# Layer 0's feed-forward and layer 1's attention of the first half, recorded as side chains of layer 0's attention

## The chip, the cores and the metric

The kernel runs on 1 core of one Trainium2 chip. The metric is the time of one execution on the device in microseconds (us); a figure without further words is the median of nine runs. A core has five engines with queues of their own: PE multiplies matrices (its weight loads are counted apart, as PEld), DVE works on vectors, ACT evaluates functions, POOL does general work and here issues indirect transfers, SP issues plain transfers. The working memory of 128 partitions is SBUF; PE writes into PSUM, from where DVE or ACT take the products.

## The reference

A sequence model of four layers in post-layernorm form: x becomes layernorm(x + attention(x)), then layernorm(x + feed-forward(x)), four times. x has 4 rows of 1024 steps of 128 numbers, in float32. Each layer has another attention and another feed-forward. The change touches the first half of these steps:

- Layer 0's attention projects x to values, a gate and a score (`in_proj`), runs a causal convolution of four taps along the sequence over them, takes the running sums along the sequence of exp(score), and of exp(score) times cosine and sine of value times four frequencies, with a decay for each of 32 heads; it divides the sums by the running sum of exp(score), scales each step by its root mean square, mixes with W_re and W_im, multiplies with the gate and projects out.
- Layer 0's feed-forward quantizes x and a weight to a 6-bit grid, each block of 32 numbers with a scale of its own, and multiplies:

```python
        scales = jnp.maximum(jnp.max(jnp.abs(blocks), axis=-1) / FP6_E2M3_MAX, eps)
        q = _nearest_on_grid(blocks / scales[..., None], _GRID)
```

  The result is (quantized x) times (quantized weight) transposed, plus a bias.
- Layer 1's attention is a diagonal complex recurrence along the sequence: an input product with B, a scan for the real and the imaginary part, an output product with C.
- Layer 1's feed-forward is a mixture of 16 experts. The router gives each token four experts out of the two best of four groups; their outputs are summed by weight, and a shared expert is added.

Layers 2 and 3 follow with a softmax attention, eight experts, a Toeplitz mixing and sixteen experts.

## The kernel before

x stays in SBUF as 32 tiles of 128 tokens by 128 numbers. The sequence is cut into four quarters of 256 steps; a quarter holds the steps of all four rows, so 1024 columns or eight tiles, and quarters depend on one another only through carried sums. Quarters 0 and 1 are the first half, called part `a`; quarters 2 and 3 are part `r` in layer 1.

`all` (from L1887) records the program. Its stages are written as generators which yield estimated costs. `run` records one to its end. `mix(main, side, pace, drain)` records a step of `main`, then as many steps of `side` as the yielded costs of `main` allow; the side's costs are multiplied by `pace` first, so that with 0.6 more of the side is recorded for the same step of `main`; with `drain` what is left of the side follows. Each instruction recorded from the side is tied (`queued`) behind the latest instruction of `main` on its engine. `chain` puts generators one after the other, `abreast` advances several together, `when` yields 1.0 at a time until a condition holds. A scheduler then fixes the order of every engine's queue while the program is built; on the chip an engine runs its queue in this order, and an instruction that waits holds up all behind it.

Up to the first experts the order of the stages is: layer 0's attention of quarters 0 and 1 (`l0_attn`), the set-up of layer 1's attention and of layer 2, the filling of layer 1's lists with zeros (`zero_lists`, transfers on SP), layer 0's feed-forward of quarters 0 and 1 (`l0_ffn`), layer 1's attention of both (`l1_attn`), the routing of these 2048 tokens (`l1_route`), then layer 0's attention of quarters 2 and 3 with the spread as its side. The spread (`spread`, L1313) is 64 indirect transfers issued by POOL (L1301): each scatters one tile of 128 tokens into the list of one of its four choices, at rows that `posl1a` names. After that the shared expert (`l1_shared`, which adds into x, and so waits for the scatters that read the same tiles of x) and the experts (`l1_experts`: L1332 fetches four tiles of a list on SP and waits for all 64 scatters; `gu` are its first products, `hg` its gated products at L1749) are mixed with layer 0's feed-forward and layer 1's attention of quarters 2 and 3. Then 64 gathers, again L1301, bring the experts' rows back as `yt`, and the kernel goes on to layer 2.

Within `l0_attn`, `prepare` forms `z` (projection and convolution as four accumulated products, psz at two buffers of two banks) and ACT turns it into values `xv`, gate `gate` and exponentials `pq`; `den` is the scan of the exponentials (L363). For each of four frequencies ACT makes cosine and sine, DVE multiplies and scans (`re`, `s`), and PE mixes the sums into `yv`. At the end DVE takes the reciprocal `rs` (L462), multiplies with the gate, and adds the product `po` to x; `norm` follows. `z2`, `ms` and `po` use the pool `side` of PSUM, two buffers for all. `quantize` (L477) works on 128x1024 numbers of a quarter with DVE (ri, st, r, dst) and POOL (v, d twice). In `l0_ffn` POOL adds the bias to x (L529), PE transposes the quantized tiles and multiplies, DVE adds into x. `l1_attn` takes half of its products with `pw` on POOL for the first half of the sequence (L667) and on DVE for the second. `norm` finds 1/sqrt with ACT's root and DVE's reciprocal (`by="act"`) or with an iteration on DVE (`by="dve"`); the second half's calls use the latter.

Of the kernel before, what the change touches and what calls it, by code (L numbers as in the profile page):

```python
# [15 lines left out]
ALU = mybir.AluOpType  # L16
# [4 lines left out]
P = 128  # L21
# [53 lines left out]
class Kernel:  # L75
# [291 lines left out]
    def l0_attn(self, qs):  # L367
# [6 lines left out]
        with ExitStack() as ctx:  # L374
            bp = self.pool(ctx, "l0b", 2)
            tp = self.pool(ctx, "l0t", 2)
            psz = self.pool(ctx, "l0z", 2, space=PSUM)
            psy = self.pool(ctx, "l0y", 1, space=PSUM)
            pss = self.side

            def prepare(q):
                z2 = self.tile(pss, [P, BLK], "s")[:, :TQ]
                for k in range(CK):
# [44 lines left out]
            for q in qs:  # L428
                xv, gate, den, pq = made.pop(q)
                ms = self.tile(pss, [P, BLK], "s")[:, :TQ]  # L430
                self.l0_by_head(ms, self.headd, den, True, False)
                yv = self.tile(psy, [P, QC], "yv")
                for m in range(MF):

                    t = self.tile(tp, [P, QC], "t")
                    nc.scalar.activation(t, xv, AF.Copy, scale=self.turn[:, m : m + 1])
                    k = self.tile(tp, [P, QC], "k")
                    nc.scalar.activation(k, xv, AF.Identity, scale=self.turn[:, m : m + 1], bias=self.rnd)
                    nc.vector.scalar_tensor_tensor(k, k, RND, t, ALU.subtract, ALU.subtract)
                    im = self.tile(tp, [P, QC], "im")  # L440
                    nc.scalar.activation(im, k, AF.Sin, scale=-2.0 * PI_IN)
                    nc.scalar.activation(k, k, AF.Abs)
                    re = self.tile(tp, [P, QC], "re")
                    nc.scalar.activation(re, k, AF.Sin, scale=-2.0 * PI_IN, bias=self.halfpi)
                    for part, v in ((1, im), (0, re)):
                        tt(v, v, pq, ALU.mult)
                        s = self.tile(tp, [P, QC], "s", bufs=3)
                        self.l0_scan(s, v, 2 * m + part, q)
                        sq = self.tile(tp, [P, QC], "sq")
                        nc.scalar.activation(sq, s, AF.Square)  # L450
                        first, last = m == 0 and part == 1, m == MF - 1 and part == 0
# [14 lines left out]
                for g in range(2):  # L466
                    po = self.tile(pss, [P, 4, D], "s")
                    for k in range(4):
                        t = g * 4 + k
                        self.mm(po[:, k, :], gate[:, t * P : (t + 1) * P], self.w_out)  # L470
                    t0 = q * QT + g * 4
                    tt(x[:, t0 : t0 + 4, :], po, x[:, t0 : t0 + 4, :], ALU.add)
                self.norm(self.quarter(q), by="act")
                yield (10.0,)


    def quantize(self, tp, dst, src, nblk):  # L477
# [10 lines left out]
        v = new()  # L488
        nc.gpsimd.tensor_tensor(v3(v), v3(src), ri.unsqueeze(2).to_broadcast(big), ALU.mult)

# [6 lines left out]

        d = new()
        nc.gpsimd.tensor_tensor(d, r, v, ALU.subtract)
        nc.vector.scalar_tensor_tensor(d, d, 2.0, st, ALU.mult, ALU.is_ge)  # L500
        nc.gpsimd.tensor_tensor(d, d, st, ALU.mult)
        nc.vector.tensor_tensor(r, r, d, ALU.subtract)
        nc.vector.tensor_tensor(v3(dst), v3(r), sc.unsqueeze(2).to_broadcast(big), ALU.mult)

    def l0_ffn(self, qs, beside=False):

        nc, tc, x = self.nc, self.tc, self.x
        with ExitStack() as ctx:
            tp = self.pool(ctx, "l0ft", 4, right=beside)
            qp = self.pool(ctx, "l0fq", 2, right=beside)  # L510
            ps = self.side if beside else self.pool(ctx, "l0fps", 2, space=PSUM)
            tag = lambda t: "s" if beside else t
            if qs[0] == 0:
                w = self.load(qp, self.ins["l0_w"])
                self.quantize(tp, w, w, D // 32)
                self.l0_wT = self.tile(self.l0, [P, D], "wT")
                self.transposes(ps, self.l0_wT, [w], tag=tag("tp"))
            for q in qs:
                t0 = q * QT
                xd = self.tile(qp, [P, QT, D], "xd")  # L520
                self.quantize(
# [6 lines left out]

                nc.gpsimd.tensor_tensor(  # L529
                    x[:, t0 : t0 + QT, :], x[:, t0 : t0 + QT, :],  # L530
                    self.row["l0_b"].unsqueeze(1).to_broadcast([P, QT, D]), ALU.add,
                )
                for g in range(2):
                    xdT = self.tile(qp, [P, BLK], "xdT")
                    self.transposes(ps, xdT, [xd[:, g * 4 + k, :] for k in range(4)], tag=tag("tp"))
                    po = self.tile(ps, [P, 4, D], tag("po"))
                    for k in range(4):
                        self.mm(po[:, k, :], xdT[:, k * P : (k + 1) * P], self.l0_wT)
                    s = slice(t0 + g * 4, t0 + g * 4 + 4)
                    nc.vector.tensor_tensor(x[:, s, :], po, x[:, s, :], ALU.add)  # L540
                    yield (4.0,)
                self.norm(self.quarter(q), by="dve" if beside else "act")
                yield (6.0,)
                for g in range(2):
                    self.turned(ps, t0 + g * 4, tag=tag("tp"))
                yield (4.0,)
# [76 lines left out]

    def l1_attn(self, qs, beside=False):
        nc, tc, x, xT = self.nc, self.tc, self.x, self.xT
# [4 lines left out]
        with ExitStack() as ctx:  # L630
            tp = self.pool(ctx, "l1t", 2, right=beside)
            ps = self.side if beside else self.pool(ctx, "l1ps", 2, space=PSUM)
            tag = lambda t: "s" if beside else t
            for q in qs:
                pu = []
                for h in range(2):
                    z = self.tile(ps, [P, BLK], tag("pu"))
                    self.mm(z, self.l1_b, xT[:, q * QC + h * BLK : q * QC + (h + 1) * BLK])
                    pu.append(z.rearrange("p (b t) -> p b t", b=B // 2))
                g = []  # L640
                for r in range(2):
# [4 lines left out]
                    if q:  # L646
                        tt(rows(b)[:, :, 0], rows(b)[:, :, 0], lh[:, r, :], ALU.add)
                    s = self.tile(tp, [P, QC], f"g{r}")
                    nc.vector.tensor_tensor_scan(
# [16 lines left out]

                (tt if beside else nc.gpsimd.tensor_tensor)(rows(g[0]), rows(g[0]), steps(pw[:, 0, :]), ALU.mult)  # L667
                tt(rows(g[1]), rows(g[1]), steps(pw[:, 1, :]), ALU.mult)
                for h in range(2):
                    po = self.tile(ps, [P, 4, D], tag("po"))  # L670
                    for k in range(4):
# [5 lines left out]
                    yield (3.0,)  # L677
                self.norm(self.quarter(q), by="dve" if beside else "act")
                yield (6.0,)
                for h in range(2):  # L680
                    self.turned(ps, q * QT + h * 4, tag=tag("tp"))
                yield (4.0,)
# [1204 lines left out]
    def all(self):  # L1887
# [259 lines left out]
```

## Time and profile before

| | |
|---|---|
| median of 9 runs | 2054.12 us (2047.82 to 2056.29) |
| the profiled execution | 2056.79 us, of which the profile's span is 2055.0 us, at a mean granted clock of PE of 0.87 |
| busy in the span: PE, PEld | 1542.0 us (75%), 935.0 us (45%) |
| DVE, ACT, POOL | 1263.8 us (62%), 823.9 us (40%), 728.4 us (35%) |

The part that the change touches is the first 610 us. By stretches of the span, with busy times in us:

| stretch (us) | what runs | PE | DVE | ACT | POOL |
|---|---|---|---|---|---|
| 0 to 31.5 | loads, set-up | 20.1 | 24.4 | 14.4 | 10.3 |
| 120 to 140.4 | end of attention, quarter 1 | 9.5 | 10.9 | 3.1 | 0 |
| 241 to 280 | layer 1's attention and routing, start of quarter 2 | 29.1 | 29.7 | 23.5 | 8.6 |
| 361.8 to 381.6 | end of attention, quarter 3 | 9.3 | 10.3 | 3.0 | 15.1 |
| 505 to 610 | gathers, the second half's feed-forward and attention | 64.9 | 67.2 | 27.7 | 69.0 |

The stretches that are left out, attention of quarters 0 and 1 (31.5 to 120), the feed-forward (140.4 to 197.5), layer 1's attention (197.5 to 241), attention of quarters 2 and 3 (280 to 361.8), the shared expert (381.6 to 425.2) and the experts (425.2 to 505), stand among the lines of the prediction. A busy time near the stretch's length says that the engine had work throughout; the rest is waiting. In a line of the timeline the first number is the start in the span, the second the duration; then come engine, source line, operation, the tile written and the tiles read with their shapes, and in brackets the idle time before it and what ended it. A "x8" at the end says that eight like instructions in a row are drawn together.

### The profile page before, as it was taken

Reading aid. Unit: us, or ns where it says so; the run is one execution under the profiler, and the core shown is the slowest. Engines: PE = TensorE matmul, PEld = TensorE weight load, DVE = VectorE, ACT = ScalarE, POOL = GpSimd, SP = SyncE. Lnnn points to the kernel's source line nnn. Section 1 sums busy time; section 2 is a strip of 40 time slices with the busy share of each in tenths; the row PEclk is TensorE's granted clock in tenths of the full one; section 3 lists DMA queues with packets and bytes.
Section 4 is the critical chain, followed back from the end, with each engine's and each line's share of the span. In section 5 each row is a group of like instructions: output and inputs, shape, how many; then the busy total and the mean of one; then the engine's idle time right before and its main releaser. Section 6 shows DMA issues by size and latency. Waiting matters only on the chain. (4 is left out here: it accounts for less than half of the span.)

```text
span 2055.0 us, 27036 instructions
## 1 busy us (share of the span) xinstructions
PE 1542.0 (75%) x9017; PEld 935.0 (45%) x9017; DVE 1263.8 (62%) x3630; ACT 823.9 (40%) x1180; POOL 728.4 (35%) x681
## 2 busy tenths in 40 slices
PE   7743777687948787989979797987989898368080
PEld 3322533376524344866633332335656686255070
DVE  8876699456766765636646676476563475347253
ACT  6821177133324443423347565662222254233050
POOL 2012168403650570174332000300247500755755
PEclk9876688799978997999989999998999899689595
DMA  9980000233440112532230000003151331232252
GB/s 310 288 233 0 0 27 34 91 103 124 134 164 33 49 67 95 182 118 70 69 129 24 1 1 1 22 1 144 47 210 69 106 117 34 79 107 67 75 157 58
DMA packets 215530, 187.10 MB, mean 91 GB/s; under 512 B 16528, under 2 KB 194064, under 8 KB 214864
## 3 DMA queue, kind: packets, MB, share of 16 engines
q1 hardware_dynamic: 194672, 142.29, 21.9%
q0 software_dynamic: 20704, 42.86, 6.4%
q8 instruction: 84, 1.38, 0.3%
q14 instruction: 70, 0.57, 0.1%
HBM read 88.49 MB, written 96.60 MB: 90 GB/s over the span
## 5 line engine op out<-in xcount | busy, mean ns | idle before, releaser
L1055 ACT ACTIVATE pr<-sc 128x1024 f32<-128x1024 f32 x288 | 279.1, 1021 | 214.8 <-PE sc L157 214.7
L157 PE MATMUL sc<-qm,kT 32*128 32x512 f32 (+3 forms) x1536 | 190.1, 549 | 0.9 <-ACT pr L1055 0.9
L157 PE MATMUL gu<-ld,xgT 128*128 x640 | 168.8, 408 | 26.5 <-DVE hg L1749 22.6
L157 PE MATMUL s<-pr,va 128*32 128x512 f32 (+3 forms) x1536 | 162.1, 518 | 19.7 <-DVE x L993 7.2
L157 PE MATMUL gu<-wall,xgT 128*128 x304 | 146.6, 607 | 2.7 <-ACT xgT L167 2.0
L157 PEld LDWEIGHTS gu<-ld,xgT 128*128 128x128 f32 x640 | 123.0, 203 | 52.6 <-DVE hg L1749 21.4
L1061 DVE TENSOR_TENSOR pr<-pr,ld 128x512 f32<-128x512 f32 (+1 forms) x160 | 92.2, 580 | 85.3 <-ACT pr L1055 84.8
L165 PE MATMUL tp<-ld,xg 128*128 128x128 f32 x396 | 66.7, 297 | 85.0 <-DMA xg<-l3rc 49.5
L157 PEld LDWEIGHTS sc<-qm,kT 32*128 32x128 f32 x1536 | 83.5, 193 | 93.6 <-issue 63.1
L1749 DVE TENSOR_TENSOR hg<-sg,gu 128x256 f32<-128x256 f32 x160 | 65.8, 417 | 93.8 <-ACT sg L1748 93.2
L167 ACT COPY xgT<-tp 128x512 f32<-128x512 f32 x99 | 57.9, 585 | 163.1 <-PE tp L165 163.1
L169 DVE COPY hT<-tp 128x512 f32<-128x512 f32 x118 | 80.9, 685 | 68.6 <-PE tp L165 68.5
L1301 POOL DMA_INDIRECT l1ra<-x,posl1a x64 | 93.0, 1454 | 59.5 <-DVE posl1a L1276 40.2
L1748 ACT ACTIVATE sg<-gu 128x256 f32<-128x256 f32 x160 | 61.0, 384 | 121.7 <-PE gu L157 96.8
L165 PE MATMUL tp<-ld,hg 128*128 128x128 f32 x624 | 98.0, 277 | 7.1 <-DVE hT L169 3.6
L165 PEld LDWEIGHTS tp<-ld,hg 128*128 128x128 f32 x624 | 78.2, 142 | 54.2 <-issue 32.5
L1507 ACT ACTIVATE sg<-gu 128x512 f32<-128x512 f32 x76 | 45.4, 598 | 139.3 <-PE gu L157 130.5
L1301 POOL DMA_INDIRECT l1rr<-x,posl1r x64 | 65.9, 1029 | 99.3 <-DVE posl1r L1276 80.1
L165 PEld LDWEIGHTS tp<-ld,xg 128*128 128x128 f32 x396 | 50.3, 153 | 90.2 <-issue 59.7
L157 PEld LDWEIGHTS s<-pr,va 128*32 128x32 f32 x1536 | 36.6, 112 | 119.4 <-issue 71.6
L157 PE MATMUL yp<-ld,hT 128*128 x640 | 87.5, 278 | 1.5 <-DVE sv L694 0.9
L1301 POOL DMA_INDIRECT yt<-l1ya,posl1a x64 | 69.0, 1079 | 51.2 <-DMA l1ya<-yg 22.0
(440 smaller groups left out, 3414.6 us busy)
## 6 DMA issues: line engine op xcount, KB each, us to landing
wall<-wall SPq DMA_DIRECT2D x16, 768.0 KB, 7.3
l3ra<-zero SPq DMA_DIRECT2D x1, 6144.0 KB, 25.2
ld<-in_l_w SPq DMA_DIRECT2D x2, 3072.0 KB, 11.9
wall<-we SPq DMA_DIRECT2D x24, 256.0 KB, 2.0
ld<-in_l_w SPq DMA_DIRECT2D x1, 6144.0 KB, 22.2
l1ra<-zero SPq DMA_DIRECT2D x1, 5120.0 KB, 20.2
l1rr<-zero SPq DMA_DIRECT2D x1, 5120.0 KB
xg<-l3ra SPq DMA_DIRECT2D x20, 256.0 KB, 2.8
```

Of the source, the lines that this page charges most:

```text
L157: return self.nc.tensor.matmul(out, lhsT, rhs, start=start, stop=stop)
L165: nc.tensor.transpose(pt[:, k * P : (k + 1) * P], s, self.ident)
L167: nc.scalar.copy(dst, pt[:, : n * P])
L169: nc.vector.tensor_copy(dst, pt[:, : n * P])
L1055: nc.scalar.activation(pr, sc[h], AF.Exp)
L1061: nc.vector.tensor_tensor(d, d, cst["tril"].unsqueeze(1).unsqueeze(1).to_broadcast([P, 2, n, P]), ALU.mult)
L1301: ins = self.nc.gpsimd.indirect_dma_start(**kw)
L1507: nc.scalar.activation(sg, gu[:, 0, :], AF.Silu)
L1748: nc.scalar.activation(sg, pg[:, :, 0, :], AF.Silu)
L1749: nc.vector.tensor_tensor(h[:, 2 * c : 2 * c + 2, :], sg, pg[:, :, 1, :], ALU.mult)
```

## The change

In `all`, `l1_setup` moves ahead of layer 0's attention. The attention of quarters 0 and 1 gets a side chain: once quarter 0 is done (the new name "l0 0" in `listed`), layer 0's feed-forward and layer 1's attention of quarter 0. The attention of quarters 2 and 3 gets a longer one than before: feed-forward and layer 1's attention of quarter 1, the routing of the first half and the spread, at pace 0.6.

For this the stages no longer share PSUM or SBUF. `l0_ffn` and `l1_attn` always use the pool `side` and the right side of SBUF; layer 0's attention leaves `side` and takes `z2`, `ms` and `po` from its own pool, one buffer each (`z2` and `po` share one), and `z` has one buffer instead of two. Several tiles lose their second buffer: `t`, `xd`, `g0`, `g1`; `l0ft` has three buffers instead of four, and in `quantize` `d` is written over `v`. The operations of POOL in `quantize`, in `l0_ffn` (the bias) and in `l1_attn` go elsewhere: the three in `quantize` and the product with `pw` to DVE, the bias to PE, which starts each product with a row of ones times the bias. The argument `beside` becomes `by`, which only chooses the way of the norm: "act" for quarters 0 and 1, "dve" for 2 and 3, as before.

```diff
@@ l0_attn
-            psz = self.pool(ctx, "l0z", 2, space=PSUM)
+            psz = self.pool(ctx, "l0z", 1, space=PSUM)
             psy = self.pool(ctx, "l0y", 1, space=PSUM)
-            pss = self.side
...
-                z2 = self.tile(pss, [P, BLK], "s")[:, :TQ]
+                z2 = self.tile(psy, [P, BLK], "po")[:, :TQ]
...
-                ms = self.tile(pss, [P, BLK], "s")[:, :TQ]
+                ms = self.tile(psy, [P, BLK], "ms")[:, :TQ]
...
-                    t = self.tile(tp, [P, QC], "t")
+                    t = self.tile(tp, [P, QC], "t", bufs=1)
...
-                    po = self.tile(pss, [P, 4, D], "s")
+                    po = self.tile(psy, [P, 4, D], "po")
...
                 self.norm(self.quarter(q), by="act")
+                self.listed.add(f"l0 {q}")
                 yield (10.0,)
@@ quantize
-        nc.gpsimd.tensor_tensor(v3(v), v3(src), ri.unsqueeze(2).to_broadcast(big), ALU.mult)
+        nc.vector.tensor_tensor(v3(v), v3(src), ri.unsqueeze(2).to_broadcast(big), ALU.mult)
...
-        d = new()
-        nc.gpsimd.tensor_tensor(d, r, v, ALU.subtract)
+        d = v
+        nc.vector.tensor_tensor(d, r, v, ALU.subtract)
         nc.vector.scalar_tensor_tensor(d, d, 2.0, st, ALU.mult, ALU.is_ge)
-        nc.gpsimd.tensor_tensor(d, d, st, ALU.mult)
+        nc.vector.tensor_tensor(d, d, st, ALU.mult)
...
@@ l0_ffn
-    def l0_ffn(self, qs, beside=False):
+    def l0_ffn(self, qs, by="dve"):
...
-            tp = self.pool(ctx, "l0ft", 4, right=beside)
-            qp = self.pool(ctx, "l0fq", 2, right=beside)
-            ps = self.side if beside else self.pool(ctx, "l0fps", 2, space=PSUM)
-            tag = lambda t: "s" if beside else t
+            tp = self.pool(ctx, "l0ft", 3, right=True)
+            qp = self.pool(ctx, "l0fq", 2, right=True)
+            ps = self.side
...
-                xd = self.tile(qp, [P, QT, D], "xd")
+                xd = self.tile(qp, [P, QT, D], "xd", bufs=1)
...
-                nc.gpsimd.tensor_tensor(
-                    x[:, t0 : t0 + QT, :], x[:, t0 : t0 + QT, :],
-                    self.row["l0_b"].unsqueeze(1).to_broadcast([P, QT, D]), ALU.add,
-                )
                 for g in range(2):
...
-                    po = self.tile(ps, [P, 4, D], tag("po"))
+                    po = self.tile(ps, [P, 4, D], "s")
                     for k in range(4):
-                        self.mm(po[:, k, :], xdT[:, k * P : (k + 1) * P], self.l0_wT)
+                        self.mm(po[:, k, :], self.cst["all1"][0:1, :], self.row["l0_b"][0:1, :], True, False)
+                        self.mm(po[:, k, :], xdT[:, k * P : (k + 1) * P], self.l0_wT, False, True)
...
-                self.norm(self.quarter(q), by="dve" if beside else "act")
+                self.norm(self.quarter(q), by=by)
...
@@ l1_attn
-    def l1_attn(self, qs, beside=False):
+    def l1_attn(self, qs, by="dve"):
...
-            tp = self.pool(ctx, "l1t", 2, right=beside)
-            ps = self.side if beside else self.pool(ctx, "l1ps", 2, space=PSUM)
+            tp = self.pool(ctx, "l1t", 2, right=True)
+            ps = self.side
...
-                    s = self.tile(tp, [P, QC], f"g{r}")
+                    s = self.tile(tp, [P, QC], f"g{r}", bufs=1)
...
-                (tt if beside else nc.gpsimd.tensor_tensor)(rows(g[0]), rows(g[0]), steps(pw[:, 0, :]), ALU.mult)
+                tt(rows(g[0]), rows(g[0]), steps(pw[:, 0, :]), ALU.mult)
...
-                self.norm(self.quarter(q), by="dve" if beside else "act")
+                self.norm(self.quarter(q), by=by)
...
@@ all
                 self.l2_wr = self.load(lgp, self.ins["l2_wr"])
-                self.run(self.l0_attn((0, 1)))
                 self.l1_setup()
+                listed = lambda name: lambda: name in self.listed
+                behind = self.chain(self.when(listed("l0 0")), self.l0_ffn((0,), "act"), self.l1_attn((0,), "act"))
+                self.run(self.mix(self.l0_attn((0, 1)), behind))
                 self.l2_setup()
                 self.zero_lists("l1")
-                self.run(self.l0_ffn((0, 1)))
-                self.run(self.l1_attn((0, 1)))
-
-                self.run(self.l1_route(a))
-                self.run(self.mix(self.l0_attn((2, 3)), self.spread("l1", a, K1)))
+                behind = self.chain(
+                    self.l0_ffn((1,), "act"), self.l1_attn((1,), "act"), self.l1_route(a), self.spread("l1", a, K1)
+                )
+                self.run(self.mix(self.l0_attn((2, 3)), behind, 0.6))
                 self.zero_lists("l2", "l3")
...
-                    side = self.chain(self.l0_ffn((2, 3), True), self.l1_attn((2, 3), True))
+                    side = self.chain(self.l0_ffn((2, 3)), self.l1_attn((2, 3)))
...
-            listed = lambda name: lambda: name in self.listed
...
```

More of the change, by code (lines that the diff above doesn't have):

```diff
@@ L516, in l0_ffn @@
                 self.l0_wT = self.tile(self.l0, [P, D], "wT")
-                self.transposes(ps, self.l0_wT, [w], tag=tag("tp"))
+                self.transposes(ps, self.l0_wT, [w], tag="s")
             for q in qs:
                 t0 = q * QT
-                xd = self.tile(qp, [P, QT, D], "xd")
+                xd = self.tile(qp, [P, QT, D], "xd", bufs=1)
                 self.quantize(
@@ L527, in l0_ffn @@
                 yield (10.0,)
-                nc.gpsimd.tensor_tensor(
-                    x[:, t0 : t0 + QT, :], x[:, t0 : t0 + QT, :],
-                    self.row["l0_b"].unsqueeze(1).to_broadcast([P, QT, D]), ALU.add,
-                )
                 for g in range(2):
                     xdT = self.tile(qp, [P, BLK], "xdT")
-                    self.transposes(ps, xdT, [xd[:, g * 4 + k, :] for k in range(4)], tag=tag("tp"))
-                    po = self.tile(ps, [P, 4, D], tag("po"))
+                    self.transposes(ps, xdT, [xd[:, g * 4 + k, :] for k in range(4)], tag="s")
+                    po = self.tile(ps, [P, 4, D], "s")
                     for k in range(4):
-                        self.mm(po[:, k, :], xdT[:, k * P : (k + 1) * P], self.l0_wT)
+                        self.mm(po[:, k, :], self.cst["all1"][0:1, :], self.row["l0_b"][0:1, :], True, False)
+                        self.mm(po[:, k, :], xdT[:, k * P : (k + 1) * P], self.l0_wT, False, True)
                     s = slice(t0 + g * 4, t0 + g * 4 + 4)
@@ L541, in l0_ffn @@
                     yield (4.0,)
-                self.norm(self.quarter(q), by="dve" if beside else "act")
+                self.norm(self.quarter(q), by=by)
                 yield (6.0,)
                 for g in range(2):
-                    self.turned(ps, t0 + g * 4, tag=tag("tp"))
+                    self.turned(ps, t0 + g * 4, tag="s")
                 yield (4.0,)
@@ L630, in l1_attn @@
         with ExitStack() as ctx:
-            tp = self.pool(ctx, "l1t", 2, right=beside)
-            ps = self.side if beside else self.pool(ctx, "l1ps", 2, space=PSUM)
-            tag = lambda t: "s" if beside else t
+            tp = self.pool(ctx, "l1t", 2, right=True)
+            ps = self.side
             for q in qs:
@@ L636, in l1_attn @@
                 for h in range(2):
-                    z = self.tile(ps, [P, BLK], tag("pu"))
+                    z = self.tile(ps, [P, BLK], "s")
                     self.mm(z, self.l1_b, xT[:, q * QC + h * BLK : q * QC + (h + 1) * BLK])
@@ L665, in l1_attn @@
                     tt(lh[:, 1, :], v[:, 1, :], u[:, 1, :], ALU.add)
-                (tt if beside else nc.gpsimd.tensor_tensor)(rows(g[0]), rows(g[0]), steps(pw[:, 0, :]), ALU.mult)
+                tt(rows(g[0]), rows(g[0]), steps(pw[:, 0, :]), ALU.mult)
                 tt(rows(g[1]), rows(g[1]), steps(pw[:, 1, :]), ALU.mult)
                 for h in range(2):
-                    po = self.tile(ps, [P, 4, D], tag("po"))
+                    po = self.tile(ps, [P, 4, D], "s")
                     for k in range(4):
@@ L677, in l1_attn @@
                     yield (3.0,)
-                self.norm(self.quarter(q), by="dve" if beside else "act")
+                self.norm(self.quarter(q), by=by)
                 yield (6.0,)
                 for h in range(2):
-                    self.turned(ps, q * QT + h * 4, tag=tag("tp"))
+                    self.turned(ps, q * QT + h * 4, tag="s")
                 yield (4.0,)
```

## The prediction

> **What bounds the kernel now.** I first read the slices of the page: in the first fifth DVE is the fullest engine, POOL has gaps. The chain of waits is of no use here: it goes back only to 2039.92 us. So I read the busy times by stage, then the timelines of DVE, POOL, SP and PE up to 610 us.
>
> ```profile
> 31.50:120.00 88.50, 68.00 (x292) 28.31 (x292) 81.73 (x88) 69.71 (x83) 0.00 (x0) 0.87 1.03 289
> 140.40:197.50 57.10, 17.62 (x72) 13.02 (x73) 34.21 (x91) 5.55 (x11) 20.19 (x11) 0.59 0.07 21
> 197.50:241.00 43.50, 25.23 (x104) 20.28 (x102) 33.90 (x82) 2.36 (x5) 6.54 (x2) 0.62 0.00 0
> 280.00:361.80 81.80, 63.04 (x287) 26.93 (x289) 79.44 (x95) 57.83 (x64) 69.30 (x42) 0.90 0.09 33
> 381.60:425.20 43.60, 30.08 (x117) 19.74 (x117) 19.07 (x23) 5.95 (x10) 9.46 (x4) 0.77 0.18 67
> 425.20:505.00 79.80, 70.89 (x469) 63.10 (x468) 53.76 (x143) 31.65 (x67) 9.47 (x4) 0.99 0.37 110
> ```
>
> Columns: stretch, length, busy time of PE, PE's weight loads, DVE, ACT, POOL (with counts), clock, DMA. Layer 0's attention (31.5 to 120, 280 to 361.8) fills DVE to 92 and 97%. Between them the feed-forward and layer 1's attention leave DVE idle for 22.9 + 9.6 us. That idle time is what the change can fill.
>
> ```profile
> 123.40 1.75 DVE L462 RECIPROCAL rs<-rs 128x256 f32<-128x256 f32 x1 [3.09 <-ACT rs L461]
> 281.65 2.28 DVE L363 TENSOR_TENSOR_SCAN den<-keep,z 128x1024 f32<-128x1024 f32 x1
> 359.51 2.27 DVE L363 TENSOR_TENSOR_SCAN s<-keep,re 128x1024 f32<-128x1024 f32 x1
> 379.36 2.20 DVE L209 TENSOR_SCALAR x<-x,mv,rstd 128x128 f32<-128x128 f32 x8
> ```
>
> ```profile
> 269.23 1.12 POOL L1301 DMA_INDIRECT l1ra<-x,posl1a  x1 [40.25 <-DVE posl1a L1276]
> ...
> 294.37 2.97 POOL L1301 DMA_INDIRECT l1ra<-x,posl1a  x1 [0.30 <-issue]
> ...
> 379.25 0.95 POOL L1301 DMA_INDIRECT l1ra<-x,posl1a  x1 [0.30 <-issue]
> 380.51 0.96 POOL L1301 DMA_INDIRECT l1ra<-x,posl1a  x1 [0.30 <-issue]
> ...
> 505.58 1.00 POOL L1301 DMA_INDIRECT yt<-l1ya,posl1a  x1 [21.98 <-DMA l1ya<-yg]
> ```
>
> ```profile
> 412.25 22.39 SPq L1332 DMA_DIRECT2D xg<-l1ra  x7
> ```
>
> ```profile
> 425.20 3.66 PE L157 MATMUL gu<-ld,xgT 128*128 x12
> ```
>
> The reader is to see that the spread (64 scatters on POOL) runs from 269.2 to 381.5, just as long as the attention of quarters 2 and 3 (DVE ends it at 381.6): it costs nothing. The experts start at 425.2, 44 us behind it, held by the shared expert. Its list was ready 30 us before SP fetched it (412.25).
>
> **The change, worked out.** Engines run queues whose order is fixed when the program is built, so I walked along the built order of the changed kernel with starts taken from rows of this trace. The built orders are the same again from the gather of yt on, so what counts is when the experts start and how long they take.
>
> *Operations moved.* In `quantize` three products go from POOL to DVE. Row L502 (DVE, 128x1024) is 1.23 us, 1.13 from start to start; POOL took 2.0 to 2.95. Two quarters: 6.8 us more on DVE, with the weights 0.8, with the product of g[0] (L667, POOL 3.27) 2 x 1.13: 10 us. The bias goes from POOL (2.34 to 2.85 us, beside DVE) to 8 matmuls a quarter: four like them (s<-wT,xdT, x8 in the records) took 1.13 us, so 2.3 us of PE a quarter, hidden under DVE except in the experts' stage.
>
> *Up to 134 us.* With one z buffer the gate's projection of quarter 0 waits for ACT's xv (24.0), the spread of pw for the gate: pq starts at 35.4, not 31.5. The waits in 31.5:120 (88.5 - 81.7 = 6.8 us) absorb that: at 106.9 both kernels are through quarter 0's norm. Then 12.9 us of attention are left, the weights' and quarter 0's quantization (2.6 + 10.7) go between them, 0.9 of waiting: the reciprocal of quarter 1 comes at 134 instead of 123.4.
>
> *134 to 198.* Tail of quarter 1, the rest of feed-forward 0, attention 0 of layer 1, first steps of quarter 2: 45 us of DVE instructions, and waits of 19: 3.4 for the transposes, copy and products of the feed-forward, 1.4 for layer 1's input product, 4.2 for its output products, 9 because z and the z2/po slot are single (po of quarter 3's z2 waits for DVE, z behind it on PE takes 7 us, ACT's gate and the spread follow in line), 1 for ACT's roots. The scan of den comes at 198, before at 281.65: 84 us gained.
>
> *198 to 326.* Before, this scan to the end of the last one took 361.8 - 281.65 = 80.2. Beside it now: quantization 11.8, add and norm 5.6, layer 1's products, scans, carries 10.6, add and norm 5.6, routing up to its weights 11.5: 45 us of DVE, which was 97% full, so all of it counts; 2.5 for waits. The last scan ends at 326: 36 us gained.
>
> *The spread.* Here the gain goes. In the built order posl1a, for which the first scatter waits, stands on DVE behind the last scan and the last reciprocal: 10 us of routing later, 336.5. Nothing of the 64 scatters lies beside the attention any more; nothing but 15 us of its tail and the shared expert (some 44 us) covers them. POOL has nothing else to do, but behind it wait SP (the experts' lists) and DVE: each of the shared expert's four adds into x waits for 16 more scatters, and hs and feed-forward 2 stand behind them. Price of one scatter: 1.26 us from start to start where DVE does the tail (15 in 362.85:381.5), (362.85 - 269.23)/49 = 1.91 beside full DVE, and in the gather (505.6:604, DVE busy 63%) (98.3 - 10.4)/64 = 1.37. Bounds 81 and 122 us; I take 1.33, as DVE will be about 43% busy with the quantization among it: 85. So the last is issued at 421.8; landing 2, the last add and xd 1.8, fetch, transposes and copies 3: the experts start at 428.5, 3.3 late.
>
> *The experts' stage* (79.8 us, PE 70.9): 8 bias matmuls beside it, 1 us after cover, and quarter 3's quantization with 3 x 1.13 more on DVE, where the hg products wait for it; POOL's operations no longer slow DVE (L493 took 2.72 beside L529, else 0.68). I take +3 in all, bounds 0 and 6.
>
> *Loads.* l0_w goes ahead of the zero fills on SP (0.33 us, 64 KB), l1_wr and l2_w behind them, used long after: nothing. The norms by ACT: 30 table loads before the shared expert, 25 before; 5 x 1.28 = 6.4 us on ACT, which has 24 us to spare in 81.8: nothing but the waits counted.
>
> Sum: +3.3 + 3 = **+6.3 us**. The profiled execution took 2056.79 (span 2055.0), 2.7 above the median of 2054.12; I add to the median: **2060.5**.
>
> [...] Beside full DVE a scatter took up to 2.97 us, else 0.96. [...]
>
> And on the tables: ACT 52.54 loads for 1.28 and activates at 53.83. The Trainium skill (ScalarE: Activation LUTs, "What ACT_TABLE_LOAD costs") adds a drain of 1.38 to each switch; no record here shows it. By the page the five loads are 13 us of ACT, an estimate, still within the 24; the sum stays.
>
> **The rivals.**
> - *POOL is starved* (slower still): scatters at 1.6 to 1.91 us, 102 to 122: +17 to 37, 2077 to 2098. For it: 1.91 measured beside scans. Against it: no scans in that window.
> - *The DVE walk is too slow* (not slower): my 19 us of waits from 134 to 198 are half that, because PE runs at full clock and z returns sooner. Then t = 326 is 317, the experts start at 419, and with 3 us in their stage it is 2051; with undisturbed scatters (81) 2047. It decides from 4 us less on. For it: the waits are at clocks of 0.6 in this trace. Against it: each link of that chain is in line.
> - *The spread is covered after all*: the experts wait for the shared expert as now. The tail would end 26 us early (326 + 29.5 = 355.5 against 381.6): 2054.1 - 26 + 3 = 2031. Against it: the order on DVE. It needs 43 us less of scatters, not possible at 0.96 each.
> - *Both cancel*: within 4 us of 2054.
>
> **How the numbers follow.** A difference under 0.2% (4.1 us) can't be told from none. Forecast (2058 to 2073) 0.50, starved POOL 0.12: slower 0.62. Cancel 0.18. DVE walk too slow 0.16 and spread covered 0.04: faster 0.20. The forecast's own range is 2054 to 2071 (walk ±6, scatters ±4, experts ±3). For 8 in 10 I leave out the covered spread, the last 3 us of the fast walk and most of the starved POOL: 2046 to 2078.
>
> **What would show it.** Right: den's scan of quarter 2 near 198, last attention scan near 326, first scatter near 337 and the 64 in 85 us, PE nearly idle before gu, experts from about 428; from the gather on all shifted alike. Wrong: the first scatter long before the last scan; gu ahead of the last scatter; DVE idle for over 30 us in all between 134 and 326, or under 8.

## The result, and the profile after

The changed kernel takes 2077.82 us (median of 10 runs, 2072.44 to 2086.83) against 2053.61 for the kernel before (31 runs on the same chip): 24.2 us more, a ratio of 1.0121, 95% interval 1.0105 to 1.0138. The profiled execution took 2075.38 us, its span 2073.4. The forecast of 2060.5 has the sign and the mechanism, but only a quarter of the size: 6.3 us. The measured time lies above the forecast's own range (2054 to 2071) and just inside the upper end of the range given for 8 in 10 (2046 to 2078).

The busy times by stage of the changed kernel (columns as in the prediction: PE, PE's weight loads, DVE, ACT, POOL, clock, DMA), cut at quarter 1's reciprocal, den's scan of quarter 2, the end of the last scan, the spread, the experts and the first gather:

```profile
136.70:208.90 72.20, 55.69 (x224) 33.67 (x224) 43.04 (x123) 20.01 (x24) 0.00 (x0) 0.74 0.12 33
208.90:342.40 133.50, 99.05 (x384) 49.69 (x384) 121.53 (x258) 75.03 (x84) 0.00 (x0) 0.81 0.00 1
350.60:433.20 82.60, 33.63 (x120) 21.47 (x119) 31.16 (x64) 6.36 (x10) 63.35 (x64) 0.67 0.24 93
433.20:444.80 11.60, 8.33 (x29) 6.43 (x30) 2.46 (x3) 1.17 (x2) 0.00 (x0) 0.50 0.33 96
444.80:529.10 84.30, 77.81 (x493) 67.65 (x492) 55.62 (x152) 31.71 (x67) 0.03 (x1) 0.99 0.35 103
```

The third row is the trade that the prediction described: 82.6 us in which PE and DVE are 41 and 38% busy, and only POOL works on. The timelines of DVE and of POOL give its two ends:

```profile
208.88 2.28 DVE L363 TENSOR_TENSOR_SCAN den<-keep,z 128x1024 f32<-128x1024 f32 x1
...
306.81 0.69 DVE L471 TENSOR_TENSOR x<-po,x 128x512 f32<-128x512 f32 x1 [8.28 <-PE po L157]
...
340.11 2.28 DVE L363 TENSOR_TENSOR_SCAN s<-keep,re 128x1024 f32<-128x1024 f32 x1
...
350.17 0.13 DVE L1271 TENSOR_SCALAR posl1a<-pm 128x64 uint32<-128x64 f32 x1
...
413.61 0.69 DVE L821 TENSOR_TENSOR x<-py,x 128x512 f32<-128x512 f32 x1 [13.64 <-DMA l1ra<-x,posl1a]
...
434.59 0.69 DVE L821 TENSOR_TENSOR x<-py,x 128x512 f32<-128x512 f32 x1 [16.16 <-DMA l1ra<-x,posl1a]
```

```profile
350.59 1.12 POOL L1296 DMA_INDIRECT l1ra<-x,posl1a  x1 [328.02 <-DVE posl1a L1271]
...
432.19 0.96 POOL L1296 DMA_INDIRECT l1ra<-x,posl1a  x1 [0.30 <-issue]
```

The attention ends 19 us earlier than before (its last scan at 342.4 instead of 361.8), but the first scatter comes at 350.6 instead of 269.2 and the last at 432.2 instead of 380.5. The shared expert's last two adds into x wait 13.64 and 16.16 us for scatters. The experts start at 444.8, 19.6 us later than the 425.2 of before, and the first gather at 529.1, 23.5 later than 505.6. From there to the end the two executions take 1549.4 (before) and 1544.3 us: nothing of the loss comes later.

### The profile page after: what moved, and what is told of

Read it like the earlier page. It is cut to its first block, busy times and chain, and to the rows that moved or that the text cites. A ratio compares the mean times of both kernels' runs of the same rounds, so it can differ in the third digit from the quotient of the medians.

```text
span 2073.4 us, 27141 instructions
## 1 busy us (share of the span) xinstructions
PE 1569.8 (76%) x9081; PEld 946.3 (46%) x9081; DVE 1266.3 (61%) x3647; ACT 831.4 (40%) x1185; POOL 651.8 (31%) x660
## 5 line engine op out<-in xcount | busy, mean ns | idle before, releaser
L1296 POOL DMA_INDIRECT l1ra<-x,posl1a x64 | 63.4, 990 | 347.2 <-DVE posl1a L1271 328.0
L1743 ACT ACTIVATE sg<-gu 128x256 f32<-128x256 f32 x160 | 61.2, 385 | 123.3 <-PE gu L157 80.0
L157 PE MATMUL yv<-s,wbd 128*128 128x512 f32 x128 | 75.5, 715 | 33.7 <-DVE s L363 33.7
```

The lines of the kernel that those rows point to most:

```text
L157: return self.nc.tensor.matmul(out, lhsT, rhs, start=start, stop=stop)
L1296: ins = self.nc.gpsimd.indirect_dma_start(**kw)
L1743: nc.scalar.activation(sg, pg[:, :, 0, :], AF.Silu)
```

## The experiments

Three theories were set against each other. A: the spread, which lies wholly behind the last scan, sets the experts' start, and the walk to the last scan is slower than forecast because of the bias matmuls. B: the single buffers of memory and PSUM make the change slow. C: the work added to DVE does.

Chips differed. On the chips of e8 to e10 the kernel before takes 2054.89 us, as at the result; on those of all other runs it takes 2397 to 2399 us, and the traces there have waits, described at the end, that those of the result's chip lack. Verdicts therefore compare a kernel with the kernel before on its own chip, or two kernels on one chip. The ratios come with their interval; the difference of two medians can lie a few us beside them. Up to the last scan the stages agree on all chips within 5 us: it ends at 342.4, 341.1 and 337.4 us in three executions of the changed kernel.

**e1 and e11: the bias with 128 rows.**

```diff
-self.mm(po[:, k, :], self.cst["all1"][0:1, :], self.row["l0_b"][0:1, :], True, False)
+self.mm(po[:, k, :], self.ident, self.row["l0_b"], True, False)
```

The product of the identity with the bias in every row is the same number. The order of instructions is the changed kernel's on every engine.

> The bias matmuls multiply with the identity (128 rows) instead of one row of ones; nothing else moves on any engine. Theory A (the walk to the last scan was longer than forecast because matmuls of one row between matmuls of 128 rows take 0.72 us each where the products alone took 0.32 us a piece, in line with the spread of 1/rms for quarter 1's gate): gate product of quarter 1 some 4 us earlier than 150.9, den's scan of quarter 2 some 7 us earlier than 208.9, 3 us more before the experts: 2068 us. Theory B (the single buffers of z and po make the walk long) and theory C (the work added to DVE does): no change, 2078 us within 4.

e1 took 1.0105 (1.0061 to 1.0148) of the kernel before. Its den scan came at 200.2, against 210.4 in e2 on the same chip, which is the changed kernel up to there; quarter 1's gate product at 147.2 against 151.8; the last scan ended at 328.7 against 340.2. Expected were 4 us at the gate and 7 at den, and they were 4.6 and 10.2. The changed kernel itself was not run on this chip; on two others where the kernel before takes as long it took 1.0159 and 1.0180.

**e2 and e12: half the spread.**

```diff
-            for i in range(k):
+            for i in range(k // 2 if lay + part.name == "l1a" else k):
```

> Leaves out 32 of the 64 scatters of the first half (third and fourth choice of every token), nothing else. Theory A (the spread, wholly behind the last scan, sets the experts' start): the last scatter lands 41 us earlier, then the shared expert's own chain is the bound, experts at about 415 instead of 444.8: 2048 us, 2040 to 2058. Theories B and C (something else sets the experts' start): within 4 us of 2078.

e2 took 1.0006 (0.9983 to 1.0028), as theory A has it (2040 to 2058 us is 0.993 to 1.002 of the kernel before at the result); the experts started at 420.8, not at 415. On another chip the changed kernel (c1) took 1.0159 (1.0130 to 1.0188), more than the 1.2% expected:

> The changed kernel once more, beside the runs of this call, to have its stages on the same chip. Every theory: 1.2% over the kernel before, first gather some 23 us later than there.

**The two edits side by side.** Since these runs lay on several chips, both edits were run once more, alone and together, on one chip with the changed kernel.

> The changed kernel beside the next three on one chip. If the chip is like that of the result: 24 us over the kernel before, experts near 445, first gather near 529. If it is like that of the first runs, where the shared expert is held up beside the spread: 42 us over it.

> The bias matmuls with 128 rows alone. Theory A: last scan 12 us earlier than in the changed kernel as on the other chip, all after it shifted alike, and 3 us less in front of the experts: 12 to 16 us below the changed kernel. Rival (the walk does not matter, since the experts wait for something else): no change in the time though the last scan comes earlier.

> Leaves out 32 of the 64 scatters of the first half alone. Theory A: the last scatter 41 us earlier; the shared expert, from 375, then ends near 400 and the experts start near 412: 28 to 36 us below the changed kernel, so 4 to 12 below the kernel before. Rival: no change.

> Both edits (leaves out the same 32 scatters). Theory A: the two lie one behind the other on the same path, so they add up: 40 to 52 us below the changed kernel. Rival (each hides the other): as much as the larger of the two alone.

| one chip | median, us | ratio to before (95%) | den, q2 | last scan ends | experts | first gather |
|---|---|---|---|---|---|---|
| c2, the change | 2435.99 | 1.0180 (1.0128 to 1.0231) | 207.7 | 337.4 | 456.7 | 541.2 |
| e11, bias of 128 rows | 2418.61 | 1.0087 (1.0058 to 1.0116) | 201.8 | 330.2 | 447.1 | 526.3 |
| e12, half the spread | 2397.16 | 1.0000 (0.9979 to 1.0022) | 208.2 | 339.2 | 420.7 | 506.6 |
| e13, both | 2374.83 | 0.9930 (0.9886 to 0.9974) | 203.0 | 331.4 | 410.6 | 490.1 |

Alone the edits are worth 17.4 and 38.8 us by the medians, together 61.2, about their sum (56.2); by the ratios it is 22, 43 and 60. All three are more than expected (12 to 16, 28 to 36, 40 to 52), but e12 does not lie below the kernel before, as it should have. The two lie one behind the other on the path that sets the end, and neither hides the other. The rivals named for these runs fall. This chip prices the exposed spread higher than that of the result (39.2 us over the kernel before, not 24.2), so the shares are its own. Buffers and work on DVE are the changed kernel's in all four, so theories B and C explain none of these differences. That e12 and e13 are no slower than the kernel before does not refute them by itself, as both leave out work that it does; e5 and e6 test them directly.

The reason lies in PE's timeline. First the products of a whole quarter in the kernel before (x16 records, two for each of eight products), then the changed kernel on the result's chip, where each product has a bias matmul ahead of it, then e11:

```profile
186.27 2.50 PE L157 MATMUL po<-wT,xdT 128*128 128x128 f32 x16
```

```profile
141.32 1.22 PE L157 MATMUL z<-rs,ld 128*128 128x256 f32 x2
142.34 0.63 PE L157 MATMUL s<-wT,xdT 128*128 128x128 f32 x2
142.90 0.79 PE L157 MATMUL s<-rows,ld 1*128 1x128 f32 x2
143.62 0.80 PE L157 MATMUL s<-wT,xdT 128*128 128x128 f32 x2
144.35 0.79 PE L157 MATMUL s<-rows,ld 1*128 1x128 f32 x2
145.07 0.80 PE L157 MATMUL s<-wT,xdT 128*128 128x128 f32 x2
...
149.67 1.22 PE L157 MATMUL z<-rs,ld 128*128 128x256 f32 x2
```

```profile
144.02 0.64 PE L157 MATMUL s<-rows,ld 128*128 128x128 f32 x2
144.45 0.63 PE L157 MATMUL s<-wT,xdT 128*128 128x128 f32 x2
...
148.35 0.39 PE L157 MATMUL s<-rows,ld 128*128 128x128 f32 x2
148.57 0.39 PE L157 MATMUL s<-wT,xdT 128*128 128x128 f32 x2
```

From start to start a matmul takes 0.72 us where shapes alternate, and 0.43 in the same place with one shape, both at a clock of about 0.5; once the clock is up it is 0.22 with one shape. PE's weight loads of the changed kernel show the gap:

```profile
142.90 0.50 PEld L157 LDWEIGHTS s<-rows,ld 1*128 1x128 f32 x2 [0.22 <-issue]
143.62 0.50 PEld L157 LDWEIGHTS s<-wT,xdT 128*128 128x128 f32 x2 [0.23 <-issue]
```

Each load starts with the matmul that it serves, 0.22 us after the end of the load before; in e11 the loads follow one another without a gap, ahead of their matmuls. The Trainium skill (TensorEngine Tiling (Array Packing), section "Key Properties") says that a change of the tiling mode drains TensorE. The trace is in accord with that: where 1*128 and 128*128 alternate, no load starts ahead of its own matmul. That a matmul of one row counts as another mode is not shown by any run here.

DVE waits for both kinds of product, first in the changed kernel, then in e11:

```profile
147.35 0.69 DVE L536 TENSOR_TENSOR x<-s,x 128x512 f32<-128x512 f32 x1 [7.85 <-PE s L157]
150.93 1.23 DVE L463 TENSOR_TENSOR gate<-z,gate 128x1024 f32<-128x1024 f32 x1 [1.77 <-PE z L157]
155.70 0.69 DVE L536 TENSOR_TENSOR x<-s,x 128x512 f32<-128x512 f32 x1 [2.28 <-PE s L157]
```

```profile
146.62 0.69 DVE L536 TENSOR_TENSOR x<-s,x 128x512 f32<-128x512 f32 x1 [5.27 <-PE s L157]
148.35 1.20 DVE L463 TENSOR_TENSOR gate<-z,gate 128x1024 f32<-128x1024 f32 x1
150.72 0.68 DVE L536 TENSOR_TENSOR x<-s,x 128x512 f32<-128x512 f32 x1
```

The clock adds to it. In the changed kernel the windows of the two groups, and in e11 the same, have:

```profile
138.50:146.90 8.40, 8.02 (x24) 5.54 (x25) 1.00 (x1) 0.59 (x1) 0.00 (x0) 0.55 0.78 221
146.90:155.50 8.60, 8.60 (x27) 6.20 (x27) 4.26 (x11) 0.59 (x1) 0.00 (x0) 0.50 0.00 0
```

```profile
140.30:146.20 5.90, 5.88 (x23) 5.10 (x24) 1.04 (x1) 0.58 (x1) 0.00 (x0) 0.50 0.80 227
146.20:149.70 3.50, 3.50 (x28) 3.13 (x27) 3.05 (x11) 0.58 (x1) 0.00 (x0) 0.99 0.00 0
```

The first group, at about half clock in both, shows the alternation alone: 8.4 us against 5.9. In e11 the second group already runs at a clock of 0.99, in the changed kernel still at 0.50, so it takes 3.5 instead of 8.6 us. The edit decides this too. Read in stretches of 0.25 us, the clock is above 0.9 in e1, e11 and e13 some 4.8 to 6.3 us after the first matmul that spreads 1/rms; in the five executions that have the changed kernel's order up to there (the result, c1, c2, e2, e12) only from 19.0 to 22.0 us after it, though in the result's trace PE is busy for 23.6 of the 24 us from that matmul on. What about the alternation keeps the clock down, the gaps or the single rows, these runs do not separate.

**e5 and e6: one part of the change alone, in the kernel before.**

```diff
-psz = self.pool(ctx, "l0z", 2, space=PSUM)
+psz = self.pool(ctx, "l0z", 1, space=PSUM)
...
-z2 = self.tile(pss, [P, BLK], "s")[:, :TQ]
+z2 = self.tile(psy, [P, BLK], "po")[:, :TQ]
```

> The kernel before with only the memory and PSUM edits to layer 0's attention (one z, one z2/po, one ms, one t); stages, order and operations as before. Theory A (spread exposed, bias matmuls slow): the single buffers cost 3 to 9 us over the kernel before. Theory B (they make the change slow): 15 us or more.

e5 (`ms`, `po` and `t` as in the change too) took 2406.46 against 2399.2 us: 1.0015 (0.9993 to 1.0036). The medians lie 7 us apart, the ratio says 4, and the interval takes in none. Theory B falls for these buffers; those of the feed-forward and of layer 1's attention were not tested alone.

```diff
-nc.gpsimd.tensor_tensor(d, d, st, ALU.mult)
+nc.vector.tensor_tensor(d, d, st, ALU.mult)
...
+self.mm(po[:, k, :], self.cst["all1"][0:1, :], self.row["l0_b"][0:1, :], True, False)
```

> The kernel before with only the moved operations (three products of the quantization and the product of g[0] on DVE, bias as matmuls of one row on PE); stages, order and buffers as before. Theory A: the chain of the feed-forward gets shorter by the faster products (POOL 2.0 to 2.9 us, DVE 1.2) and longer by the bias matmuls (8 pairs a quarter, 0.7 us each in place of nothing): within 5 us of the kernel before. Theory C (the work added to DVE makes the change slow): 10 us or more above it.

e6 (all moved operations) took 2401.47: 1.0010 (0.9989 to 1.0031). Theory C falls. In e6 a gain and a loss seem to cancel: the experts start at 418.9 us, where the profile of the kernel before has 425.2, but their stage takes 86.5 us, where that profile has 80.4 and e5, without the bias matmuls, 79.9. The profile of the kernel before is of another chip; that the faster quantization on DVE makes the gain was not tested alone.

**e3, e4 and e7: the routing earlier.** All keep the overlap of the first half and move the routing on DVE ahead of some of the scans.

```diff
 e3
-self.run(self.mix(self.l0_attn((2, 3)), behind, 0.6))
+self.run(self.l0_ffn((1,), "act"), self.l1_attn((1,), "act"), self.l1_route(a))
+self.run(self.mix(self.l0_attn((2, 3)), self.spread("l1", a, K1)))
 e4
...
+self.run(self.mix(ahead, self.l0_attn((2, 3)), 4.0))
 e7
...
+self.run(self.mix(self.l0_attn((0, 1, 2)), behind, 0.6, False))
+self.run(self.mix(self.chain(behind, self.l1_route(a), self.spread("l1", a, K1)), self.l0_attn((3,)), 2.0))
```

> Feed-forward, layer 1's attention and routing of quarter 1 are recorded ahead of attention 2 and 3, and only the spread beside it; the first half's overlap stays. On DVE the routing's result then stands ahead of the last 6 of quarter 3's scans. Theory A: first scatter near 310 instead of 350.6, about 18 scatters beside the scans at 1.9 us, 46 at 1.3: last near 405, experts near 418: 2051 us. Theory B: the buffers are the same, no change: 2078. Theory C: same work on DVE, no change: 2078.

> Main and side change places in the second stage: feed-forward, layer 1's attention, routing of quarter 1 and the spread are the main, attention of quarters 2 and 3 the side at pace 4. On DVE the routing's result then stands behind 3 of the attention's 18 scans. Theory A: first scatter near 245, all 64 beside the attention as in the kernel before (1.9 us each while DVE is full), so the shared expert is the bound again, behind an attention that ends near 362: experts near 412, 2045 us, below the kernel before by about 9. Theory B or C: as many single buffers and as much DVE work as in the changed kernel, not under 2070.

> Attention of quarters 0, 1 and 2 as one main with feed-forward and layer 1's attention of quarters 0 and 1 as its side, not drained; then routing and spread as the main and attention of quarter 3 as the side; the bias as one matmul of 128 rows for four tiles. On DVE the routing's result stands ahead of all 8 scans of quarter 3. Theory A: first scatter near 275, 24 of them beside quarter 3's scans at 1.9 us, 40 at 1.3: last near 371, experts near 385, 40 us earlier than in the kernel before: 2015 us, 2005 to 2030. Theory B or C: buffers and DVE's work are the changed kernel's, so not under 2060.

They took 1.0064 (1.0038 to 1.0091), 1.0044 (1.0015 to 1.0073) and 1.0004 (0.9982 to 1.0026): less than the change's 1.0159 and 1.0180 on such chips, but none of them below the kernel before, and the forecasts of 2051, 2045 and 2015 us were all wrong. Two reasons are in the traces. The first scatter came at 306, 278 and 298 us, where 310, 245 and 275 were expected, so late in e4 and e7: with the attention moved into the gaps DVE is the bound (e7: 200.6 of 236 us from 120 to 356), while in e4 DVE is busy for only 94.1 of 141 us from 136 to 277 and waits 28.7 us for PE's products in quarters that go one at a time. And the shared expert was held up beside the spread, in a wait that only these chips show: its first add in e3 came at 404.2, after 32.4 us put down to "remote", though the tail of the attention ended at 357.5.

**e8 to e10: leave the first half alone and fill its gaps.** e8 records attention 0 and 1 without a side; then feed-forward and layer 1's attention of both quarters, routing and spread are the main, and the attention of quarters 2 and 3 is the side. Three products of the quantization go back to POOL, and the bias is one matmul of 128 rows for four tiles.

```diff
+self.run(self.l0_attn((0, 1)))
+ahead = self.chain(
+    self.l0_ffn((0, 1), "act"), self.l1_attn((0, 1), "act"), self.l1_route(a), self.spread("l1", a, K1)
+)
+self.run(self.mix(ahead, self.l0_attn((2, 3)), 4.0))
...
+self.mm(po, self.ident, self.row["l0_b"].unsqueeze(1).to_broadcast([P, 4, D]), True, False)
```

> Attention of quarters 0 and 1 alone, as in the kernel before; then feed-forward and layer 1's attention of quarters 0 and 1 together, routing and spread as the main, attention of quarters 2 and 3 as the side at pace 4; quantization on POOL, the bias as one matmul of 128 rows for four tiles. On DVE the routing's result stands behind 3 of the 18 scans. Theory A: first scatter near 270 as in the kernel before (268.8), but a part of attention 2 already done in what was idle time of DVE there: last scan near 338 in place of 361.8, all scatters done near 380, experts near 400 in place of 425, 20 to 25 us below the kernel before. If the spread beside the shared expert is dear on this chip (it held the shared expert up in the runs so far): 5 to 15 below. Theory B or C: not below it.

> As the run before with pace 2: the routing's result stands on DVE behind 10 of the 18 scans. Theory A: first scatter near 290, last scan near 335, 25 scatters beside scans at 1.8 us and 39 at 1.27: last near 385, experts near 400, 15 to 25 us below the kernel before, up to 10 worse where the spread beside the shared expert is dear. Theory B or C: not below it.

> Three quarters first and quarter 3 beside the spread, with the quantization on POOL as in the kernel before. Theory A: DVE is the bound up to the routing, and it has 7 us less to do there: first scatter near 290 in place of 298, 5 to 10 us below the same kernel with the quantization on DVE, which took as long as the kernel before. Theory C the same, with 10 or more; theory B no change.

e8 took 2040.73 us against 2054.89, 0.9939 (0.9918 to 0.9960): 14 us below the kernel before, so below both kernels, but short of the 20 to 25 us expected: the last scan ends at 353.9, not near 338, and the experts start at 408.5, not near 400. e9 (pace 2.0) took 2052.14, 0.9973 (0.9949 to 0.9996), a miss: expected were 15 to 25 us below. e10 (e7 with the quantization on POOL) took 2046.77, 0.9973 (0.9952 to 0.9995); its first scatter came at 301.6 us, no earlier than the 298.3 of e7, so the small gain is not the one expected. The spread and the end of the attention in e8, on POOL and DVE:

```profile
274.68 1.12 POOL L1296 DMA_INDIRECT l1ra<-x,posl1a  x1 [106.31 <-DVE posl1a L1271]
...
378.98 0.96 POOL L1296 DMA_INDIRECT l1ra<-x,posl1a  x1 [0.30 <-issue]
```

```profile
351.59 2.29 DVE L363 TENSOR_TENSOR_SCAN s<-keep,re 128x1024 f32<-128x1024 f32 x1
```

The scatters lie beside the attention as before, which ends 8 us earlier, and the experts start 17 us earlier. In e9 the first scatter came at 302.5 and the last at 396.2; the experts waited until 418.9. In these two runs the gap filling pays only where it does not delay the routing.

## Why the prediction was wrong

| step of the forecast | forecast, us | measured, us |
|---|---|---|
| reciprocal of quarter 1 | at 134 | at 136.7 |
| from there to den's scan of quarter 2 | 64 | 72.2 |
| to the end of the last scan | 128 | 133.5 |
| to the first scatter | 10.8 | 8.2 |
| 64 scatters | 85 | 82.6 |
| last scatter to the experts | 6.7 | 11.6 |
| experts' stage | +3 | +3.9 |

The deviations up to the first gather add up to 17.2 us, the 23.5 by which it comes later less the 6.3 forecast. One of the prediction's own signs of being wrong came up: DVE is idle for 41.1 of the 205.7 us from quarter 1's reciprocal to the end of the last scan, where over 30 was named.

Four rows of PE bear on the points below. The first two, of the kernel before, hold the price that the prediction took for the bias; the others, of the changed kernel, stand ahead of a late `po`:

```profile
421.59 2.08 PE L157 MATMUL s<-wT,xdT 128*128 128x128 f32 x8 [0.68 <-ACT xdT L167]
436.07 1.13 PE L157 MATMUL s<-wT,xdT 128*128 128x128 f32 x8
```

```profile
298.03 6.85 PE L157 MATMUL s<-ld,xT 128*128 128x16 f32 x32
304.72 2.05 PE L157 MATMUL po<-ld,gate 128*128 128x128 f32 x8
```

- *The spread takes the place of the wait for DVE*: right, in place and size. It starts behind the last scan, takes 1.30 us a scatter (forecast 1.33), and halving it is worth 38.8 us on one chip. "POOL is starved" fell: no scatter took longer than 1.43 us.
- *The bias matmuls*: the step that failed. The prediction priced them like four products, "2.3 us of PE a quarter, hidden under DVE except in the experts' stage". The row behind that price (436.07) ran at a clock of 1.0; four such products at 421.59 in the same trace, at 0.5, took 2.08 us instead of 1.13. In the changed kernel the bias matmuls cost 0.72 us each at a clock of 0.5, with as much for the product beside them, and 0.41 at full clock in the experts' stage, and they were not hidden. They stand on PE between the matmuls that spread 1/rms for quarter 1's gate, for which DVE waits in line; again in front of the transposes of the experts' first rows; and in the experts' stage, where PE is the fullest engine. Between c2 and e11 the stretch from the reciprocal to den's scan shrinks from 71.7 to 63.3 us (the forecast said 64), that from the last scatter's end to the experts from 30.1 to 27.1, and the experts' stage from 84.5 to 79.2. These three make 16.7 us, where the prediction allowed 1 for the bias; the medians lie 17.4 apart. (In the two profiled executions the first gather lies 15.0 us apart and the end 9.0; that of e11 is the slowest of its runs.) Taken off the 24.2 of the result they leave some 7 where 6.3 were forecast; that is an estimate across chips, as no e11 ran on one like that of the result.
- *The experts' stage*: +3.9 where +3 was forecast, right by luck. The forecast had 1 us for the bias and the rest for the quantization; the bias alone is worth 5.3 (84.5 against 79.2 in e11), and without it the stage is no longer than the 80.4 of before (of another chip).
- *Waits from den's scan to the last scan*: "2.5 for waits" was too little. DVE waited 8.28 us for `po` at 306.8, as PE had the router products of 16 tiles (298.03) ahead of it. DVE's own work was less than forecast, 121.5 us. The 5.5 us by which this stretch is longer and the 5.0 by which the next two rows are shorter cancel by chance. The wait was seen, but no run takes it away alone.
- *The single buffers*: forecast as 9 us of the waits. Alone in the kernel before (e5) they cost 4 us by the ratio, in an interval that reaches from -2 to +9: not at odds with it, and not the cause of the miss.
- *Moved quantization and table loads*: forecast as 10 us of DVE and nothing of ACT. In the kernel before the moved operations cost nothing that can be measured (e6). No run tests the table loads alone.
- *Scatters beside the quantization*: forecast within the 1.33 us of a scatter. Four of the 64 took 1.26 to 1.43 us instead of 0.96, all while DVE worked on the quantization or the shared expert, so a delay is there, but it is at most 0.5 us for each. Beside the scans of the kernel before a scatter took up to 3.02 (the prediction read 2.97).
- *The rival "The DVE walk is too slow"* held that the waits from 134 to 198 were half of what was forecast. They were more, 29.2 us and not 19: DVE was busy for 43.0 of 72.2 us.

## What to carry to other kernels

A matmul has no price by itself: before pricing an added one by its neighbours, compare its rows and columns with theirs and the clock that they ran at, and look at what stands behind it in PE's queue. When a stage is moved into another's idle time, ask which queue loses its cover: here a gain of 19 us on DVE uncovered 82 us on POOL. Keep the step that feeds the longest serial queue at the front, and fill the gaps with the work that nobody waits for, as e8 does.

## What was not expected of the hardware

On the chips where the kernel before took some 2397 us, engines stood still beside POOL's indirect transfers. In c2, ACT and POOL show it:

```profile
376.65 0.60 ACT L734 ACTIVATE sg<-pg 128x512 f32<-128x512 f32 x1 [1.54 <-PE pg L157]
426.35 0.60 ACT L734 ACTIVATE sg<-pg 128x512 f32<-128x512 f32 x1 [49.10 <-remote]
```

```profile
425.61 0.96 POOL L1296 DMA_INDIRECT l1ra<-x,posl1a  x1 [0.31 <-issue]
```

ACT waits 49.1 us, put down to "remote", until the last scatter (the line at 425.61), and PE and DVE stand still for most of that time, until 421.6 and 414.5; the trace of the change on the result's chip has no wait put down to "remote". In e6, a kernel in the old order, DVE waited 63.1 us in the same way, until 786.6, beside the spread of layer 1's second half, whose last scatter starts at 776.6. So on these chips a spread that is not hidden costs more than its own length suggests: from the last scan's end to the experts' start c2 takes 119.3 us, the changed kernel on the result's chip 102.4. What holds the engines up stays open.
